# Seven block products for all eight expert pairs, with values read back from DRAM and gate logits laid over 128 partitions

## The chip, the core and the metric

The kernel runs on one core of a Trainium2 chip. Its engines are TensorE (PE, with its weight loads shown apart as PEld), VectorE (DVE), ScalarE (ACT), GpSimd (POOL) and SyncE (SP), which here issues every DMA. The engines run their own instructions in order and wait for each other by semaphores. SBUF is the on-chip memory with 128 partitions, PSUM the one that TensorE writes. The metric is the device time of one execution in microseconds; lower is better. Comparisons use the median of several runs and, where shown, a 95% interval.

## The reference

Eight sequences of 1,024 tokens with 256 features pass an attention layer without a softmax, a residual sum with a layer norm, and a mixture of 16 experts with a second residual sum and layer norm. All is float32. Cut to what matters:

```python
# x: (8, 1024, 256); Wqkv: (256, 768); keys: (16, 256, 128); values: (16, 128, 256)
q, k, v = split(x @ Wqkv + bqkv)
q2 = l2norm(q*q / (sum(q*q) + 1e-7), axis=-1)     # after the mean over features is taken off
k2 = l2norm(k*k / (sum(k*k) + 1e-7), axis=-2)
attn = (v + q2 @ (k2.T @ v) / sqrt(1024)) @ Wln + bln
x = layernorm(x + attn)
sel = sigmoid(x @ expert_sel.T)                    # (tokens, 16)
scores = relu(einsum('bsd,edh->bseh', x, keys))
out = einsum('bseh,ehv,bse->bsv', scores, values, sel)
x = layernorm(x + out)
```

## The kernel before

**Tiles.** The 8,192 tokens are worked in 16 chunks of 512 (`CH`). Features lie on partitions in two halves of 128. Each float32 operand is split into a high part, rounded to the type in which TensorE multiplies (`fp32r`), and the rest as a low part; a product then takes three matmuls, high by high, high by low, low by high (`passes3`). Names ending in h and l are such pairs: `ych`, `ycl` hold the input of the experts for a chunk, `keyh`, `keyl` the first layer's weights, `valh`, `vall` the second layer's, `sh`, `sl` the gated scores.

**The planner.** Nothing is written in the order in which it runs. Every operation is added with `add(engine, cost, key, fn, r, w)` as a task: a due time (`key`, about one unit for each expert), an estimate of its duration, and what it reads and writes. `Work.order` plays the program through with these costs and writes out one order for all engines; a task may start when its inputs are there, its slots are free and its key is at most `WINDOW` ahead of the oldest open task. Buffers come from slots with tags (`SB_SLOTS` in SBUF, `PS_SLOTS` in PSUM): a buffer takes a slot when the first task that touches it is placed and gives it back after the last one. At run time the engines follow that order and the semaphores. The constants `AT_...`, `EAGER`, `BOOST`, `LAG` set keys. TensorE is filled with short `warm` matmuls in the first stage where the planner has nothing for it.

**Stages.** The head makes the weights, the attention of chunk 0 and chunk 1 and the gates of the first experts. Then the steady part runs the 16 experts of chunk c, while the attention of the next chunks is worked in between: `u_y(c+1)` (queries, residual sum, gates), `u_q(c+2)`, `u_k(c+3)`, and `u_m` for the matrix of each sequence. `u_end` does the last layer norm of a chunk.

**The experts.** `u_pair(c, p)` does experts 2p and 2p+1. In the old way (`plain1`) an expert's first layer is 6 matmuls of 512 columns into one PSUM tile `h`. For chunks from 1 on and pairs in `FAST_PAIRS` (4 to 7), `fast1` computes both experts together: the two experts' keys and the two halves of the tokens are taken as a product of 2x2 blocks, which is done by seven block products in place of eight. Each product is 3 matmuls of 256 columns. It needs sums of key blocks (`sums_h`, `sums_l`, made once in `u_sums` by GpSimd) and sums of token blocks (`th`, `tl`, made for each chunk in `u_t`). The results are put together in two PSUM tiles `hx` and `hy`: products are accumulated, and ScalarE copies a partial sum from one half to another (L1099, L1100, L1103, L1106) before the next product is added; VectorE adds the last part (L1109). `gated` then does on either way: VectorE takes the maximum with zero and multiplies by the gate (L1055), ScalarE casts to the high part (L1056), VectorE subtracts for the low part (L1057). `ffn2` is the second layer, 6 matmuls of 512 columns for each expert (L1137) into two PSUM tiles that collect over all 16 experts.

**The gates.** In `u_y` the logits of 16 experts by 512 tokens are one row for each expert on 16 partitions (`gr`). The sigmoid is built of Exp, Ln and Newton steps: eight VectorE operations and six ScalarE operations on 16x512. The result is stored to DRAM (`sel`, L938), from where each expert's row is spread over 128 partitions (`selb`, L1030), two slots for two pairs.

**Slots.** Weights of experts sit in `g0` to `g3`, four slots each: key and value parts of four experts. `s4` has four slots for the split tokens and for k2 and q2, `t4` six for work tiles, among them `th` and `tl`. PSUM has four `h` slots: one tile for each expert in the old way, `hx` and `hy` for each pair in the other.

Of the kernel before, what the change touches and what calls it, by code (L numbers as in the profile page):

```python
# [15 lines left out]
P = 128  # L16
# [9 lines left out]
EARLY = 14  # L26
WARM = 14
WINDOW = 10.47
AHEAD = 120
HALVED = 4  # L30
FAST_FROM = 1
FAST_AT = 0.39
AT_Y, AT_YEND, AT_X, AT_N, AT_K, AT_Q, AT_M, AT_END = 2.04, 4.17, 0.95, 0.19, 5.21, 12, 16.28, -0.91
AT_Q1, AT_K2, AT_W1, AT_W2, AT_W3, AT_SUMS, AT_SEL = -30, -19.9, -10.93, -7.7, 8.8, 8.58, 7
EAGER = 3.73
BOOST = 2.0
RESERVE = {"att": 1}
FAST_PAIRS = range(4, 8)
# [3 lines left out]
    "ld2": 3, "xh": 2, "xl": 2, "s4": 4, "ych": 2, "ycl": 2, "sh": 2, "sl": 2, "selb": 2, "gt": 2, "t4": 6, "t2": 4,  # L42
    "v1": 2, "g0": 4, "g1": 4, "g2": 4, "g3": 4, "acc": 1, "asb": 1, "mh": 1, "ml": 1, "tiny": 14,
# [35 lines left out]
class Buf:  # L79
# [4 lines left out]
    def __getitem__(self, i):  # L84
        return self.ap[i]

# [236 lines left out]
def attn_ffn_kernel(ctx, tc, x, xT, wqT, wk, wvT, wlnT, bcols, brows, selT, keys, values, outT):  # L323
# [93 lines left out]
    keyh, keyl, valh, vall = {}, {}, {}, {}  # L417
# [99 lines left out]
    def split(c, key, name, src, h, l, width):  # L517

        rows = h.shape[1]
        n = 1 if c < 2 else 2  # L520
        for i in range(n):
            s = slice(i * rows // n, (i + 1) * rows // n)
            part = None if n == 1 else i
            b = sbuf("g3" if c < 2 else "ld2", [P, rows // n, width], f"{name}{c}_{i}")
            add("D", 2.1 / n, key, lambda b=b, s=s: nc.sync.dma_start(out=b.ap, in_=src(s)), w=[b])
            high(key + 1.2, lambda s=s: h[:, s], lambda b=b: b.ap, 2 * CH // n, [b], [(h, part)], c < 2)
            for j in range(2 // n):
                m = rows // 2
# [39 lines left out]
    def u_k(c, key):  # L568
# [5 lines left out]
        k2h[c] = h = sbuf(in_first(c, "s4", "ych"), [P, 4, D], f"k2h{c}", FR)  # L574
        k2l[c] = l = sbuf(in_first(c, "s4", "ycl"), [P, 4, D], f"k2l{c}", FR)
        for g in range(2):
# [7 lines left out]
            add("T", c_mm(D, 12), key + g, lambda g=g, t=t: project(c, g, t, wkh, wkl), r=x_parts(c, g) + [wkh, wkl], w=[t])  # L584
# [135 lines left out]
    def u_q(c, key):  # L720
        q = sbuf("t4", [P, 4, D], f"q{c}")
        s, n2, y, a = (tiny(f"{n}{c}") for n in ("qs", "qn", "qy", "qa"))
        q2h[c], q2l[c] = (sbuf("s4", [P, 2, CH], f"{t}{c}", FR) for t in ("q2h", "q2l"))
        for g in range(2):
# [7 lines left out]
            add("T", c_mm(D, 12), key + g, lambda g=g, t=t: project(c, g, t, wqh, wql), r=x_parts(c, g) + [wqh, wql], w=[t])  # L732
# [33 lines left out]
        for ct in range(2):  # L766
            o = psum(f"qt{c}_{ct}")

            def turn(ct=ct, o=o):
                for t in range(4):  # L770
                    T.transpose(o[:, t * P : (t + 1) * P], q[:, t, ct * P : (ct + 1) * P], ident.ap)  # L771

            add("T", c_mm(P, 4), key + 6.5 + ct * 0.2, turn, r=[q, ident], w=[o])
            add("S", c_act(CH, plain=True), key + 7 + ct * 0.2, lambda ct=ct, o=o: S.copy(q2h[c][:, ct, :], o.ap), r=[o], w=[(q2h[c], ct)])
            add("V", c_dve(CH), key + 7.5 + ct * 0.2, lambda ct=ct, o=o: V.tensor_tensor(
                q2l[c][:, ct, :], o.ap, f(q2h[c][:, ct, :]), ALU.subtract), r=[o, (q2h[c], ct)], w=[(q2l[c], ct)])
# [88 lines left out]
    def u_y(c, key):  # L865
# [18 lines left out]
        for jt in range(2):  # L884
            t = psum(f"yp{c}_{jt}", "h" if c == 0 else "att")
            k0 = key + jt
            add("T", c_mm(CH, 6), k0, lambda t=t, jt=jt: ymx(t, jt), r=[xh[c], xl[c], wyh, wyl] + ([] if c == 0 else [mh[b], ml[b], q2h[c], q2l[c]]), w=[t])
# [16 lines left out]
        def smm():  # L904
# [7 lines left out]
        gr = sbuf("t4", [P, 2, CH], f"gr{c}")  # L912
        a, z = lambda: gr[:NE, 0, :], lambda: gr[:NE, 1, :]
        rs = sbuf("t2", [P, CH], f"rs{c}")
        add("S", c_act(CH, plain=True), key + 0.5, lambda: S.copy(z(), z0[32 : 32 + NE, :]), r=[z0], w=[(gr, 1)])
        add("V", c_dve(CH), key + 1, lambda: V.tensor_tensor(z(), z0[:NE, :], z(), ALU.add), r=[z0, (gr, 1)], w=[(gr, 1)])

# [3 lines left out]
        key += 1.8  # L921

        add("S", c_act(CH), key, lambda: S.activation(a(), v[:NE], AF.Ln, bias=c_zero[:NE]), r=[v, c_zero], w=[(gr, 0)])
        add("S", c_act(CH), key + 0.1, lambda: S.activation(a(), a(), AF.Exp, bias=c_zero[:NE], scale=-0.5), r=[(gr, 0), c_zero], w=[(gr, 0)])
        newton(key + 0.4, lambda: v[:NE], a, lambda: rs[:NE], 1.0, [v, (gr, 0)], [rs, (gr, 0)])
        add("V", c_dve(CH), key + 0.8, lambda: V.tensor_tensor(z(), z(), a(), ALU.mult), r=[gr], w=[(gr, 1)], port=True)

        add("S", c_act(CH), key + 1.2, lambda: S.activation(z(), z(), AF.Exp, bias=c_zero[:NE], scale=-1.0), r=[(gr, 1), c_zero], w=[(gr, 1)])
        add("V", c_dve(CH, fast=True), key + 1.6, lambda: V.tensor_scalar(z(), z(), 2.0**62, 1.0, ALU.min, ALU.add),
            r=[(gr, 1)], w=[(gr, 1)], port=True)  # L930

        add("S", c_act(CH), key + 2, lambda: S.activation(a(), z(), AF.Ln, bias=c_zero[:NE]), r=[(gr, 1), c_zero], w=[(gr, 0)])
        add("S", c_act(CH), key + 2.1, lambda: S.activation(a(), a(), AF.Exp, bias=c_zero[:NE], scale=-1.0), r=[(gr, 0), c_zero], w=[(gr, 0)])
        add("V", c_dve(CH), key + 2.4, lambda: V.tensor_tensor(z(), z(), a(), ALU.mult), r=[gr], w=[(gr, 1)], port=True)
        add("V", c_dve(CH), key + 2.5, lambda: V.scalar_tensor_tensor(a(), z(), 2.0, a(), ALU.subtract, ALU.mult, reverse0=True),  # L935
            r=[gr], w=[(gr, 0)], port=True)
        selt[c] = d = work.buf("dram", [NE, CH], F32, f"sel{c}")
        add("D", 0.2, key + 2.8, lambda: nc.sync.dma_start(out=d.ap, in_=a()), r=[gr], w=[d])  # L938


    def u_weights(g, key):
        for to, name in ((keyh, "keyh"), (keyl, "keyl"), (valh, "valh"), (vall, "vall")):
            to[g] = sbuf(f"g{g}", [P, 4, 2, P] if to in (keyh, keyl) else [P, 4, D], f"{name}{g}", FR)
# [15 lines left out]
        for i in range(n):  # L959
# [10 lines left out]
            for j in range(size):  # L970
                e = here.start + j
                add("S", c_act(D), key + 1.4, lambda j=j, e=e, vst=vst, m=m: S.activation(valh[g][:, e], vst[:, j], AF.Identity, bias=m[:, j : j + 1]),
                    r=[vst, m], w=[(valh[g], e)])
                add("V", c_dve(D, ptr=True), key + 1.8, lambda j=j, e=e, vst=vst, m=m: V.scalar_tensor_tensor(
                    vall[g][:, e], vst[:, j], m[:, j : j + 1], f(valh[g][:, e]), ALU.add, ALU.subtract),
                    r=[vst, m, (valh[g], e)], w=[(vall[g], e)], port=True)
# [27 lines left out]
    def u_t(c, key):  # L1004
        yh, yl, n = ych[c], ycl[c], CH // 2
        y, u = sbuf("t4", [P, 2, CH], f"y{c}"), sbuf("t4", [P, 4, n], f"tu{c}")
        th[c], tl[c] = (sbuf("t4", [P, 4, n], f"t{i}{c}", FR) for i in "hl")
        for k in range(2):
            apply(key, lambda k=k: y[:, k], lambda k=k: f(yh[:, k]), lambda k=k: f(yl[:, k]), ALU.add, CH, [yh, yl], [(y, k)], "G")
# [5 lines left out]
        add("S", c_act(4 * n, plain=True), key + 1, lambda: S.copy(h.ap, u.ap), r=[u], w=[h])  # L1015
# [17 lines left out]
    def u_pair(c, p):  # L1033
# [3 lines left out]
        gates_of(c, p, max(0, SOON - 2 * p) if c == 0 else 0)  # L1037
        sel = selb[c, p]
# [74 lines left out]
    def ffn2_halves(c, e, key, a, b):  # L1113

        g, i = e // 4, e % 2
# [3 lines left out]
        def run(part):  # L1119
            r = slice(part * CH // 2, (part + 1) * CH // 2)  # L1120
            for j, (w, x) in enumerate(((valh[g], a), (vall[g], a), (valh[g], b))):
                for v in range(2):
                    out = rest[v][:, : CH // 2] if part else wps[c][v][:, r]
                    T.matmul(out, w[:, e % 4, v * P : (v + 1) * P], x[:, i, r], start=part == 1 and e == NE - HALVED and j == 0,
                             stop=e == NE - 1 and j == 2)

        for part in range(2):
            add("T", c_mm(CH // 2, 6), key + LAG + part * HALVED, lambda part=part: run(part),
                r=[(valh[g], e % 4), (vall[g], e % 4), (a, i), (b, i)], w=rest if part else wps[c])

    def ffn2(c, e, key, a, b):
        g, i = e // 4, e % 2

        def run():
            for j, (w, r) in enumerate(((valh[g], a), (vall[g], a), (valh[g], b))):
                for v in range(2):
                    T.matmul(wps[c][v].ap, w[:, e % 4, v * P : (v + 1) * P], r[:, i], start=e == 0 and j == 0, stop=e == NE - 1 and j == 2)  # L1137

        t = add("T", c_mm(CH, 6), key + LAG, run, r=[(valh[g], e % 4), (vall[g], e % 4), (a, i), (b, i)], w=wps[c])
# [3 lines left out]
    def u_end(c):  # L1143
# [3 lines left out]
        for v in range(2):  # L1147
            add("V", c_dve(CH), key, lambda v=v: V.tensor_tensor(w[:, v, :], wps[c][v].ap, f(ych[c][:, v, :]), ALU.add),  # L1148
                r=[wps[c][v], ych[c]], w=[(w, v)])
# [6 lines left out]
        yb = sbuf("t4", [P, 2, CH], f"wy{c}")  # L1156
# [249 lines left out]
```

## Time and profile before

| | |
|---|---|
| median of 3 runs | 1017.82 us (1015.98 to 1018.09) |
| the profiled execution, first to last instruction | 1013.8 us, mean granted TensorE clock 0.996 |
| program | 16,268 instructions |
| DMA | 99.52 MB, mean 98 GB/s, packets of the dynamic queue 30.4% of 16 engines' time |

The page of the profile gives busy time by engine, then the chain of work that ended last: it starts at the last instruction and goes back, at each step to what released it. Groups of instructions are shown as line, engine, operation, tile written <- tiles read, with a count and busy time, mean duration and the idle time before it. A matmul's duration is from its start to its modelled end and overlaps with the next, so a pace is read from starts. How much of each slice each engine was busy (digits are tenths) and the granted clock:

```profile
PE   9999999999999999999999999999999999999996
...
DVE  7889888588776887768887688867888688686775
ACT  7767576676776767767676676757776675665543
POOL 1001685538564474655636475454754537333430
PEclk9999999999999999999999999999999999999998
```

### The profile page before, as it was taken

What the parts mean: (1) busy time and instruction counts of PE and PEld (TensorE: products, weight loads), DVE (VectorE), ACT (ScalarE), POOL (GpSimd) and SP (SyncE); (2) the same over time, 40 slices, a digit from 0 to 9 for tenths busy, and PEclk for the clock granted to TensorE, in tenths of its full rate; (3) what the DMA queues carried; (4) which work ended last, traced back from release to release, by engine and by line L of the source; (5) the groups of instructions that cost most, each with busy time, mean ns of one, the idle gap of its engine ahead of it and who ended that gap; (6) DMA issues with size and microseconds to landing.
All of it is one profiled execution on the core that took longest, in us unless ns stands there. A gap on an engine that the chain in (4) does not pass through costs nothing.

```text
span 1013.8 us, 16268 instructions
## 1 busy us (share of the span) xinstructions
PE 1003.8 (99%) x5709; PEld 868.9 (86%) x5709; DVE 792.9 (78%) x1363; ACT 678.5 (67%) x1515; POOL 488.5 (48%) x436
## 2 busy tenths in 40 slices
PE   9999999999999999999999999999999999999996
PEld 9978879888898988889888888988889888888886
DVE  7889888588776887768887688867888688686775
ACT  7767576676776767767676676757776675665543
POOL 1001685538564474655636475454754537333430
PEclk9999999999999999999999999999999999999998
DMA  6144433322241333323223232323323222223131
GB/s 203 56 124 125 120 98 118 94 97 93 83 126 65 116 94 104 99 89 97 94 91 110 86 105 70 116 96 102 105 75 104 94 85 75 93 85 105 64 125 42
DMA packets 65298, 99.52 MB, mean 98 GB/s; under 512 B 6336, under 2 KB 24896, under 8 KB 65216
## 3 DMA queue, kind: packets, MB, share of 16 engines
q1 hardware_dynamic: 65216, 98.48, 30.4%
q8 instruction: 45, 0.74, 0.3%
q14 instruction: 37, 0.30, 0.1%
HBM read 89.54 MB, written 8.91 MB: 97 GB/s over the span
## 4 chain that ended last, share of the span: by engine, by line
PE 92%; DVE 3%; POOL 2%; DMA 1%; ACT 1%; issue 1%; SPq 0%; POOLq 0%; DVEq 0%; ACTq 0%
PE w L1137 32%; PE h L358 17%; PE hx L1090 11%; PE yp L358 8%; PE qp L358 4%; PE hy L1090 4%; PE kp L358 4%; PE ap L358 4%; PE qt L771 1%; PE sp L358 1%; PE pm L358 1%; DMA ksr<-keys 1%; PE warm L435 0%; DVE sl L1057 0%; DMA xf<-xT 0%
## 5 line engine op out<-in xcount | busy, mean ns | idle before, releaser
L1137 PE MATMUL w<-sh,valh 128*128 128x512 f32 x504 | 157.9, 394 | 0.0
L1137 PE MATMUL w<-sh,vall 128*128 128x512 f32 x504 | 157.8, 394 | 0.0
L1137 PE MATMUL w<-sl,valh 128*128 128x512 f32 x504 | 157.6, 394 | 0.0
L1055 DVE SCALAR_TENSOR_TENSOR h<-h,selb 128x512 f32<-128x512 f32 x136 | 93.9, 692 | 29.6 <-PE h L358 24.9
L1137 PEld LDWEIGHTS w<-sl,valh 128*128 128x128 f32 x504 | 94.6, 188 | 22.4
L1137 PEld LDWEIGHTS w<-sh,vall 128*128 128x128 f32 x504 | 94.6, 188 | 22.0
L1056 ACT CAST sh<-h 128x512 fp32r<-128x512 f32 x136 | 74.2, 588 | 57.2 <-PE w L1137 46.2
L358 PE MATMUL h<-ych,keyh 128*128 128x512 f32 x272 | 110.4, 406 | 0.0
L358 PE MATMUL h<-ycl,keyh 128*128 128x512 f32 x272 | 108.3, 398 | 0.0
L358 PE MATMUL h<-ych,keyl 128*128 128x512 f32 x272 | 107.5, 395 | 0.0
L1057 DVE TENSOR_TENSOR sl<-h,sh 128x512 fp32r<-128x512 f32 x136 | 87.7, 682 | 22.4 <-ACT sh L1056 22.3
L1137 PEld LDWEIGHTS w<-sh,valh 128*128 128x128 f32 x504 | 86.0, 188 | 10.9
L389 POOL TENSOR_TENSOR k<-k,ks 128x512 f32<-128x512 f32 x25 | 30.9, 1256 | 102.4 <-DVE ks L566 102.4
L1109 DVE TENSOR_TENSOR hx<-hx,p 128x512 f32<-128x512 f32 x60 | 41.8, 696 | 29.9 <-ACT hy L1106 29.6
L389 POOL TENSOR_TENSOR ysq<-ysq 128x512 f32<-128x512 f32 x15 | 20.0, 1333 | 89.2 <-ACT ysq L891 89.2
L1151 POOL TENSOR_TENSOR w<-w,ycl 128x512 f32<-128x512 f32 x30 | 38.3, 1297 | 49.4 <-DVE w L1148 49.4
L358 PEld LDWEIGHTS h<-ych,keyl 128*128 128x128 f32 x272 | 51.5, 189 | 12.2
L358 PEld LDWEIGHTS h<-ycl,keyh 128*128 128x128 f32 x272 | 51.6, 190 | 10.7
L358 PEld LDWEIGHTS h<-ych,keyh 128*128 128x128 f32 x272 | 51.5, 189 | 10.9
L893 DVE SCALAR_TENSOR_TENSOR ycl<-yp,by,ych 128x512 fp32r<-128x512 f32 x32 | 24.0, 750 | 41.4 <-ACT ysq L891 41.4
L389 POOL TENSOR_TENSOR kss<-kss 128x512 f32<-128x512 f32 (+1 forms) x18 | 25.0, 1391 | 57.6 <-DVE gr L935 57.6
L1057 DVE TENSOR_TENSOR sl<-hx,sh 128x512 fp32r<-128x512 f32 x60 | 40.8, 681 | 15.1 <-ACT sh L1056 14.9
(511 smaller groups left out, 3204.6 us busy)
## 6 DMA issues: line engine op xcount, KB each, us to landing
selb<-sel SPq DMA_DIRECT2D x253, 256.0 KB, 3.4
xf<-xT SPq DMA_DIRECT2D x30, 256.0 KB, 2.8
outT<-w SPq DMA_DIRECT2D x15, 512.0 KB, 3.0
nf<-x SPq DMA_DIRECT2D x28, 256.0 KB, 4.7
kst<-keys SPq DMA_DIRECT2D x6, 256.0 KB, 3.3
vst<-values SPq DMA_DIRECT2D x6, 256.0 KB, 3.0
nf<-x SPq DMA_DIRECT2D x2, 512.0 KB, 7.6
ksr<-keys SPq DMA_DIRECT2D x4, 256.0 KB, 3.6
```

The costliest lines, as they stand in the source:

```text
L358: T.matmul(out, w, r, start=first and i == 0, stop=last and i == len(terms) - 1)
L389: fns = {e: (lambda e=e: ENG[e].tensor_tensor(out(), a(), b(), op)) for e in engines}
L771: T.transpose(o[:, t * P : (t + 1) * P], q[:, t, ct * P : (ct + 1) * P], ident.ap)
L893: add("V", c_dve(CH, ptr=True), k0 + 0.9, lambda t=t, jt=jt: V.scalar_tensor_tensor(yl[:, jt, :], t.ap, by[:, jt : jt + 1], f(yh[:, jt, :] ...
L1055: add("V", c_dve(CH), key + 0.1, lambda: V.scalar_tensor_tensor(at(t.ap), at(h.ap), 0.0, out(sel), ALU.max, ALU.mult), r=[h] + reads(sel), ...
L1056: add("S", c_act(CH, plain=True), key + 0.1, lambda: S.copy(out(a), at(t.ap)), r=[t], w=reads(a))
L1057: add("V", c_dve(CH), key + 0.1, lambda: V.tensor_tensor(out(b), at(t.ap), f(out(a)), ALU.subtract), r=[t] + reads(a), w=reads(b))
L1090: T.matmul(out(), wi, ri, start=first and i == 0, stop=True, skip_group_check=True)
L1109: add("V", c_dve(CH), key + 0.09, lambda: V.tensor_tensor(halves_(x.ap), halves_(x.ap), p5.ap.to_broadcast([P, 2, n]), ALU.add), r=[x, p5] ...
L1137: T.matmul(wps[c][v].ap, w[:, e % 4, v * P : (v + 1) * P], r[:, i], start=e == 0 and j == 0, stop=e == NE - 1 and j == 2)
L1151: add("G", c_pool(CH), key + 0.5, lambda v=v: G.tensor_tensor(w[:, v, :], w[:, v, :], f(ycl[c][:, v, :]), ALU.add), r=[(w, v), ycl[c]], w= ...
```

## The change

Five things change together.

- `FAST_PAIRS` is `range(8)`: from chunk 1 on all eight pairs use `fast1`. `u_sums` makes key sums for eight pairs.
- Value weights no longer stay in SBUF. `u_weights` makes them for chunk 0 in tiles for one pair each (`vals`, tag `vs`, four slots) and stores each to DRAM (`vdram`); from chunk 1 on `u_pair` loads each pair's tile again, 512 KB, by SP. The slots of `g0` to `g3` go from four to two.
- The gate logits are moved by DMA into a tile of 128 partitions by 64 (16 experts by 8 pieces of 64 tokens), and so is the variance row `v`; the sigmoid runs on 128x64 and is stored from there.
- Slots are given out anew: `s4` becomes `nn` and `kq`, `th` and `tl` get `tf` (two slots) of their own, `t4` has four, and `u_end` uses one work tile twice. A mark `TAKE` lets a task reserve a slot that a later task writes; it adds no dependency between operations.
- The planner's constants have other values.

```diff
-EARLY = 14
+EARLY = 17.06
-WINDOW = 10.47
-AHEAD = 120
+WINDOW = 11.33
+AHEAD = 125.36
-FAST_AT = 0.39
-AT_Y, AT_YEND, AT_X, AT_N, AT_K, AT_Q, AT_M, AT_END = 2.04, 4.17, 0.95, 0.19, 5.21, 12, 16.28, -0.91
-AT_Q1, AT_K2, AT_W1, AT_W2, AT_W3, AT_SUMS, AT_SEL = -30, -19.9, -10.93, -7.7, 8.8, 8.58, 7
+FAST_AT = 8.9
+AT_Y, AT_YEND, AT_X, AT_N, AT_K, AT_Q, AT_M, AT_END = 2.49, 3.72, 6.25, -3.12, 10.31, 11.71, 15.9, -0.74
+AT_Q1, AT_K2, AT_W1, AT_W2, AT_W3, AT_SUMS, AT_SEL, AT_VALS = -31.56, -10.52, -6.89, 1.02, 6.34, 4.43, 7.02, 2.33
-BOOST = 2.0
+BOOST = 0.99
-FAST_PAIRS = range(4, 8)
+FAST_PAIRS = range(8)
 SB_SLOTS = {
-    "ld2": 3, "xh": 2, "xl": 2, "s4": 4, "ych": 2, "ycl": 2, "sh": 2, "sl": 2, "selb": 2, "gt": 2, "t4": 6, "t2": 4,
-    "v1": 2, "g0": 4, "g1": 4, "g2": 4, "g3": 4, "acc": 1, "asb": 1, "mh": 1, "ml": 1, "tiny": 14,
+    "ld2": 3, "xh": 2, "xl": 2, "nn": 2, "kq": 2, "ych": 2, "ycl": 2, "sh": 2, "sl": 2, "selb": 2, "gt": 2, "t4": 4, "tf": 2, "t2": 4,
+    "v1": 2, "g0": 2, "g1": 2, "g2": 2, "g3": 2, "vs": 4, "acc": 1, "asb": 1, "mh": 1, "ml": 1, "tiny": 14,
 }
...
+TAKE = -1
...
@@ u_y
-        add("S", c_act(CH, plain=True), key + 0.5, lambda: S.copy(z(), z0[32 : 32 + NE, :]), r=[z0], w=[(gr, 1)])
-        add("V", c_dve(CH), key + 1, lambda: V.tensor_tensor(z(), z0[:NE, :], z(), ALU.add), r=[z0, (gr, 1)], w=[(gr, 1)])
+        zc = sbuf("t2", [P, CH], f"zc{c}")
+        gt = sbuf("gt", [P, 6, CH // 8], f"gt{c}")
+        spread = lambda ap: ap.rearrange("e (t n) -> e t n", t=8)
+        eh, el, v8, a, rs, z = (lambda i=i: gt[:, i] for i in range(6))
+        m = CH // 8
+        add("S", c_act(CH, plain=True), key + 0.5, lambda: S.copy(zc[: 32 + NE], z0[: 32 + NE, :]), r=[z0], w=[zc])
+        for i in range(2):
+            add("D", 0.3, key + 0.7, lambda i=i: nc.sync.dma_start(out=gt[:, i], in_=spread(zc[32 * i : 32 * i + NE])), r=[zc], w=[(gt, i)])
...
+        add("D", 0.3, key + 1.7, lambda: nc.sync.dma_start(out=v8(), in_=spread(v[:NE])), r=[v], w=[(gt, 2)])
...
+        add("V", c_dve(m), key, lambda: V.tensor_tensor(z(), eh(), el(), ALU.add), r=[(gt, 0), (gt, 1)], w=[(gt, 5)], port=True)
+        add("S", c_act(m, 2), key, ln, r=[(gt, 2), c_zero], w=[(gt, 3)])
+        add("V", c_dve(m, 4), key + 0.2, logits, r=[(gt, 2)], w=[(gt, 3), (gt, 4), (gt, 5)], port=True)
+        add("S", c_act(m), key + 0.4, lambda: S.activation(z(), z(), AF.Exp, bias=c_zero.ap, scale=-1.0), r=[c_zero], w=[(gt, 5)])
+        add("V", c_dve(m), key + 0.5, lambda: V.tensor_scalar(z(), z(), 2.0**62, 1.0, ALU.min, ALU.add), w=[(gt, 5)], port=True)
+        add("S", c_act(m, 2), key + 0.6, inverse_, r=[(gt, 5), c_zero], w=[(gt, 3)])
+        add("V", c_dve(m, 2), key + 0.8, out, w=[(gt, 3), (gt, 5)], port=True)
         selt[c] = d = work.buf("dram", [NE, CH], F32, f"sel{c}")
-        add("D", 0.2, key + 2.8, lambda: nc.sync.dma_start(out=d.ap, in_=a()), r=[gr], w=[d])
+        add("D", 0.3, key + 0.9, lambda: nc.sync.dma_start(out=d.ap.rearrange("e (t n) -> (e t) n", t=8), in_=a()), r=[(gt, 3)], w=[d])
@@ u_weights
+        for p in (2 * g, 2 * g + 1):
+            vals[0, p] = sbuf("vs", [P, 2, 2, D], f"vals0_{p}", FR)
+            vdram[p] = work.buf("dram", [P, 2, 2, D], F32, f"vdram{p}")
...
+        for p in (2 * g, 2 * g + 1):
+            add("D", 2.1, key + 2.2, lambda p=p: nc.sync.dma_start(out=vdram[p].ap, in_=f(vals[0, p].ap)), r=[vals[0, p]], w=[vdram[p]])
@@ u_t
-        th[c], tl[c] = (sbuf("t4", [P, 4, n], f"t{i}{c}", FR) for i in "hl")
+        th[c], tl[c] = (sbuf("tf", [P, 4, n], f"t{i}{c}", FR) for i in "hl")
...
-        add("S", c_act(4 * n, plain=True), key + 1, lambda: S.copy(h.ap, u.ap), r=[u], w=[h])
+        add("S", c_act(4 * n, plain=True), key + 1, lambda: S.copy(h.ap, u.ap), r=[u], w=[h, (l, TAKE)])
@@ u_pair
+        if c:
+            vals[c, p] = sbuf("vs", [P, 2, 2, D], f"vals{c}_{p}", FR)
+            fetched[:] = [add("D", 2.1, key - AT_VALS, lambda: nc.sync.dma_start(out=f(vals[c, p].ap), in_=vdram[p].ap),
+                              r=[vdram[p]], w=[vals[c, p]], after=fetched)]
@@ ffn2
-            for j, (w, r) in enumerate(((valh[g], a), (vall[g], a), (valh[g], b))):
+            for j, (w, r) in enumerate(((0, a), (1, a), (0, b))):
                 for v in range(2):
-                    T.matmul(wps[c][v].ap, w[:, e % 4, v * P : (v + 1) * P], r[:, i], start=e == 0 and j == 0, stop=e == NE - 1 and j == 2)
+                    T.matmul(wps[c][v].ap, u[:, w, i, v * P : (v + 1) * P], r[:, i], start=e == 0 and j == 0, stop=e == NE - 1 and j == 2)
@@ u_end
-        yb = sbuf("t4", [P, 2, CH], f"wy{c}")
+        yb = sq
```

In the orders that the two programs are built to, TensorE has 816 matmuls of 512 columns of `h` before and 96 after, 1,260 of 256 columns of `hx` and `hy` before and 2,520 after, and 38 and 46 `warm` ones. SP issues 374 DMAs before and 551 after: 120 of `vals`, 8 of `vdram` and 45 of `gt` are new, and 4 more of `ksr`. Twelve halves of `tl` move from GpSimd to VectorE.

## The prediction

> **What bounds the kernel now.** I read the page's busy times and chain first, then the order of time on TensorE, then the groups and waits, last the DMA rows.
>
> ```profile
> PE 1003.8 (99%) x5709; PEld 868.9 (86%) x5709; DVE 792.9 (78%) x1363; ACT 678.5 (67%) x1515; POOL 488.5 (48%) x436
> PE 92%; DVE 3%; POOL 2%; DMA 1%; ACT 1%; issue 1%; SPq 0%; POOLq 0%; DVEq 0%; ACTq 0%
> ```
>
> The chain that ended last lies to 92% on TensorE. Busy time of pipelined matmuls says little, so I take the distance from one start to the next (first column of the order of time, us; chunk 8, a pair computed the old way, then one by block products):
>
> ```profile
> 552.88 0.39 PE L358 MATMUL h<-ych,keyh 128*128 128x512 f32 x1
> ...
> 554.04 0.39 PE L358 MATMUL h<-ych,keyl 128*128 128x512 f32 x1
> 554.27 0.63 PE L1137 MATMUL w<-sh,valh 128*128 128x512 f32 x2
> ...
> 576.02 0.28 PE L1090 MATMUL hx<-th,keyh 128*128 128x256 f32 x1
> ...
> 576.62 0.28 PE L1090 MATMUL hx<-ych,ksl 128*128 128x256 f32 x1
> 576.74 0.28 PE L358 MATMUL kp<-wkh,xh 128*128 128x256 f32 x1
> ```
>
> Six matmuls of 512 columns take 554.27-552.88 = 1.39 us, 232 ns each; six of 256 take 0.72 us, 120 ns each. Over the whole trace the starts of the second layer's 1,512 matmuls are 232.0 ns apart, and of all 5,708 distances those above the pace of their form add up to only 6.4 us, most of it before 65 us. So TensorE never waits in the steady part: the time is its work, and any TensorE work taken out comes off the span until something else is late.
>
> **The change, part by part.** *Block products.* Chunks 1 to 15 now do pairs 0 to 3 by L1090's seven products of 3 matmuls too: 15 x 4 = 60 pairs. Each loses 12 matmuls of 512 columns and gains 21 of 256. The 720 removed ones hold TensorE 169.6 us (235.5 ns each, their changes from transposes included); bare, at 232.0 ns, 167.0. The 1,260 present ones of 256 columns hold it 151.0 us (119.9 ns each, their waits included), and 60 pairs more cost the same again. Gain: 169.6-151.0 = 18.6 us; bare 16.0. I take 17, as part of the changes from transposes will fall on other matmuls.
>
> [...]
>
> *The chain inside a pair.* Between products ScalarE copies halves of PSUM, and TensorE needs other matmuls meanwhile. What one step needs (same pair of chunk 8):
>
> ```profile
> 572.70 0.28 PE L1090 MATMUL hx<-ych,keyl 128*128 128x256 f32 x1
> ...
> 573.81 0.39 PE L1090 MATMUL hx<-th,ksh 128*128 128x256 f32 x1
> ```
> ```profile
> 573.02 0.36 ACT L1099 COPY hy<-hx 128x256 f32<-128x256 f32 x1 [0.95 <-PE hx L1090]
> 573.38 0.37 ACT L1100 COPY p<-hx 128x256 f32<-128x256 f32 x1
> ```
>
> The last product starts at 572.70, ends 0.28 later, two copies follow 0.04 behind it, and the next product starts 0.06 after them: 1.11 us, so 1.11-0.12 = 1.0 us of other work hides it. Here four matmuls of 512 columns (0.93 us) lie between, and about 0.1 us shows. In the changed program's order I counted what lies there for every pair: 1.39 us at the median as before, but 0.71 to 0.76 in chunk 14 pairs 2 and 6 and chunk 15 pairs 0 and 1, and nothing in chunk 15 pair 2, where no attention work is left. That costs 4 x about 0.35 + 1.1 = 2.5 us. Bounds 1 (ScalarE is emptier there) and 5 (a 0.58 cast stands in front of each).
>
> *One set of th, tl.* They get their own two slots (tag tf), enough for one chunk, and the first pair now needs them, not the fifth. ScalarE's cast of th (L1015) waits for the last product of the old chunk, VectorE's tl follows.
>
> ```profile
> L1015 ACT CAST th<-tu 128x1024 fp32r<-128x1024 f32 x15 | 15.6, 1042 | 2.3 <-POOL tu L389 2.3
> L389 DVE TENSOR_TENSOR tl<-tu,th 128x512 fp32r<-128x512 f32 x16 | 17.3, 1089 | 1.0 <-ACT th L1015 1.0
> L389 POOL TENSOR_TENSOR tl<-tu,th 128x512 fp32r<-128x512 f32 x14 | 21.9, 1561 | 25.8 <-ACT th L1015 25.8
> ```
>
> Columns: busy us, mean ns | idle before. Counted from the start of that last product: ScalarE 0.32 to 1.36; VectorE first does hy's gate and a bias add (0.60 us apart when they follow each other), so tl's first half runs from 1.52 to 2.2, or 2.6 at 1,089 ns. In the changed order 6 matmuls of 512 and 12 of 256 columns lie between, 2.82 us, so tl is wanted at 0.12+2.82+0.12 = 3.06: hidden with 0.4 to 0.8 us over. Queued behind the cast are q's squares on ScalarE, behind tl the inverse of k's sums on VectorE, for which GpSimd's scaling of k waits; TensorE wants what comes of these only pairs later. Into chunk 15 just 1.39 us lie between: 0.32+1.04+0.04+(0.68 to 1.09)+0.06-1.63 = 0.5 to 0.9 us lost, I take 0.7. Its pair 1 also reuses PSUM 2.1 us after the pair two before has ended, where VectorE and ScalarE need 0.32 + two gates 1.2 + cast 0.58 + two subtractions 1.2, some overlapping, about 2.9: 0.8 us (0 to 2).
>
> *Other engines.* VectorE gains 60 adds (L1109, 696 ns): +42 us, and about 13 for 12 halves of tl that leave GpSimd. It loses the gate's eight operations on 16x512, 86 us in all, for eight on 128x64; these lie between the 128x4 rows (153 to 178 ns) and the 128x256 rows (471): 120 x 0.22 = 26 us, nearest the small ones. Net -5. ScalarE gains 60 x (361+371+364+358) ns = 87 us and 15 x 0.58 for zc, and loses 63 us of gate work for 75 x 0.3 = 22: net +55, to 734 us, 73%. GpSimd: -19 for tl, +15 for four more sets of key sums. None becomes the bound on average. The split of the slots (nn, kq, four of t4 for six) and the early reservations add no instruction; I cost them at nothing, since attention works one to three chunks ahead of the experts. Without that lead a late y would cost its own chain, about 2.7 us a chunk (two VectorE passes, a cast and a subtraction, 0.6 to 0.7 each).
>
> *DMA.* 120 loads of 512 KB of values, 8 stores of it, 45 small gate transfers.
>
> ```profile
> selb<-sel SPq DMA_DIRECT2D x253, 256.0 KB, 3.4
> outT<-w SPq DMA_DIRECT2D x15, 512.0 KB, 3.0
> nf<-x SPq DMA_DIRECT2D x28, 256.0 KB, 4.7
> nf<-x SPq DMA_DIRECT2D x2, 512.0 KB, 7.6
> sel<-gr SPq DMA_DIRECT2D x15, 32.0 KB, 1.7
> ```
>
> Last column: us from issue to landing. Bytes go from 99.5 to about 169 MB, 168 GB/s, with the DMA engines about half busy; the first slice already moved 203. In the changed order each load stands 14 to 29 us of TensorE work ahead of its first use and lands in 3.0 to 7.6: no cost. It waits on SP for the second layer four pairs back; behind it are the next gates (selb), issued 6 to 18 us ahead of use at 3.4 us landing. If that cover went, each late us would cost TensorE one. The small transfers of zc are issued 2.7 us or more ahead of VectorE's add, those of v1 2.1 to 3.8 (mean 2.9) ahead of ScalarE's Ln; at sel's 1.7 us they cost nothing.
>
> *Start.* Eight more warming matmuls stand in the head's order, two records of 0.112 us each: 1.8 us of further idle; bounds -2 (VectorE, 19 of 20 us busy from 20 to 40, has 7 instructions less there) and +3.5 (12 kp matmuls, 1.4 us, move behind it). I take 1.8.
>
> Sum: -17+2.5+0.7+0.8+1.8 = -11.2 us on this execution's 1013.8: 1002.6. The runs' median, 1017.8, stands 4.0 above that span, so **1007 us**. The low ends give -18.6+1+0.5+0-2 = -19.1, the high ends -16+5+0.9+2+3.5 = -4.6: its own range is 999 to 1013.
>
> **Rivals.** *The new wait takes the gain* (no change). If tl's second half counts, or VectorE is one operation late, a chunk boundary costs 1.52+1.09+1.09+0.06+0.69-3.06 = 1.4 us at most; 13 more of them cost 18: 1025 at worst, 1016 at half, which is the price I give it. For it: th and tl were ready some 30 us ahead and are not now. Against: TensorE is told of each half apart.
>
> *The gate's transfers hold ScalarE and VectorE* (slower). Both take instructions in order, so an Ln or an add waiting for 128 pieces of 256 bytes behind a 512 KB load holds the copies that the block products wait for. At nf's 4.7 us the Ln is 1.8 late, less the 0.4 that a step has over (1.39-1.0): 1.4 x 15 = 21 us, 1028. It decides from 11.2/15+0.4 = 1.1 us of lateness, a landing of 4.0 us. For it: the order leaves 2.9 us, and outT's 512 KB or a load of values goes out just before. Against: sel's 32 KB landed in 1.7. [...]
>
> *The values come late* (slower): SP in order behind a wait. One us for each eighth load is 15 us, 1022. The lead of 14 us speaks against it.
>
> **How the numbers follow.** Forecast 0.70; new wait 0.13; gate transfers 0.12; values 0.05. Within 0.2% (2 us, about what runs of this kernel can tell apart) I put 0.06, all from the new wait's half price, whose smaller prices give 0.05 of faster. Faster 0.75, slower 0.19. Range 998 to 1017: below it less than 0.05, above it most of the slower cases.
>
> **What would show it.** Right: 96 matmuls of h left, 2,520 of hx and hy at about 120 ns, no TensorE wait between chunks 2 and 14, a few us in chunk 15. Wrong: TensorE idle at each chunk's first hx on the cast of th or on tl, ScalarE's Ln on gt waiting for DMA each chunk, or w waiting for vals.

## The result and the profile after

The changed kernel takes 1024.86 us (median of 4 runs, 1023.06 to 1026.56); the kernel before, beside it on the same chip, 1016.9. The ratio is 1.0075, with a 95% interval of 1.0059 to 1.0091: slower by about 0.8%, where 1007 us was forecast. The profiled execution of the changed kernel has a span of 1021.8 us, 8.0 more than before.

From the page of the changed kernel, the busy times and the chain of work that ended last:

```profile
PE 1000.1 (98%) x6265; PEld 889.6 (87%) x6265; DVE 773.0 (76%) x1438; ACT 726.4 (71%) x1764; POOL 468.8 (46%) x444
...
PE 75%; DVE 10%; ACT 7%; DMA 5%; issue 2%; POOL 0%; SPq 0%; DVEq 0%; ACTq 0%
```

The averages moved the way that was forecast: ScalarE 726 us (734 said), VectorE 773 (788 said), no other engine near its limit. But the chain, 92% TensorE before, is 75% TensorE now; VectorE, ScalarE and DMA have come into it. TensorE is waiting again. How much, is read from the distances between the starts of its matmuls. I count as a wait what a distance has above the median of its form (232 ns for 512 columns, 118 for 256, 109 for transposes) where that is over 60 ns; sums in us, worked out from the order of time on TensorE:

| stretch of the trace | before | after | difference |
|---|---|---|---|
| start to 64 us | 8.1 | 9.0 | +0.9 |
| 64 to 160 us (chunks 0 and 1) | 1.7 | 7.5 | +5.8 |
| 160 to 935 us | 4.2 | 16.9 | +12.6 |
| 935 us to the end (chunk 15) | 1.3 | 5.4 | +4.2 |

The work itself shrank as planned: 1,260 matmuls of 256 columns at 118 ns in place of 720 of 512 at 232 ns are 148.7 - 167.0 = -18.4 us, and eight more warming matmuls +1.8. With +23.5 of waits that makes +6.9 of the 8.0. So nothing went wrong with the block products' arithmetic; the gain was paid out again in waits.

Who is waited for? In the views of waits (us in all, times, longest) only idle time after the modelled end of the matmul before counts, so the sums are smaller than the table's. The kernel before has one such wait of TensorE from 64 us to its end; most of the rest of its 7.1 us are distances about 0.1 us over the pace, without idle time:

```profile
PE hx L1090 <- ACT p L1100: 0.9, 1, 0.9
```

In the changed kernel, ScalarE's waits in the gate, and TensorE's own between 160 and 935 us and from 935 us to the end:

```profile
ACT gt L950 <- DVE gt L937: 12.8, 13, 1.3
ACT gt L932 <- DMA gt<-v: 11.3, 10, 2.2
```
```profile
PE hx L1117 <- ACT p L1127: 3.4, 7, 1.2
PE hy L1117 <- ACT hy L1133: 1.8, 3, 1.0
```
```profile
PE hx L1117 <- DVE sl L1084: 2.3, 3, 1.3
PE hy L1117 <- ACT hy L1126: 0.4, 1, 0.4
PE hx L1117 <- DVE tl L392: 0.3, 1, 0.3
```

In the steady part TensorE waits for ScalarE's copies inside the block products (L1127, L1133), and ScalarE itself has stood still in the gate, ten times for the transfer gt<-v. The DMA rows of the page say why (last column: median us from issue to landing):

```profile
selb<-sel SPq DMA_DIRECT2D x253, 256.0 KB, 3.8
vals<-vdram SPq DMA_DIRECT2D x120, 512.0 KB, 4.8
...
outT<-w SPq DMA_DIRECT2D x15, 512.0 KB, 6.6
...
gt<-zc SPq DMA_DIRECT2D x30, 32.0 KB, 2.1
...
gt<-v SPq DMA_DIRECT2D x15, 32.0 KB, 4.6
sel<-gt SPq DMA_DIRECT2D x15, 32.0 KB, 1.9
```

Three transfers have the same 32 KB; gt<-zc and sel land in about 2 us, gt<-v in 4.6 (medians). One case in the order of time, in chunk 3 (SP's queue, ScalarE, TensorE; start, us, in brackets the idle time before):

```profile
286.62 0.38 SPq L1063 DMA_DIRECT2D vals<-vdram  x1
287.10 0.39 SPq L1193 DMA_DIRECT2D outT<-w  x1
290.68 0.55 SPq L928 DMA_DIRECT2D gt<-v  x1
```
```profile
290.84 0.36 ACT L1126 COPY hy<-hx 128x256 f32<-128x256 f32 x1 [2.32 <-PE hx L1117]
...
295.28 0.35 ACT L932 ACTIVATE gt<-gt,c_zero 128x64 f32<-128x64 f32 x1 [1.77 <-DMA gt<-v]
295.67 0.35 ACT L933 ACTIVATE gt<-gt,c_zero 128x64 f32<-128x64 f32 x1
295.92 0.36 ACT L1133 COPY hy<-hx 128x256 f32<-128x256 f32 x1
```
```profile
295.46 0.28 PE L1117 MATMUL hx<-ych,keyl 128*128 128x256 f32 x1
296.33 0.39 PE L1117 MATMUL hy<-th,keyh 128*128 128x256 f32 x1 [0.60 <-ACT hy L1133]
```

512 KB of values and 512 KB of output were issued 4.1 and 3.6 us ahead of gt<-v on the same queue. ScalarE stands 1.77 us at Ln (L932), and the copy of L1133, which has nothing to do with the gate, comes behind it; TensorE's next step starts 296.33-295.46-0.12 = 0.75 us late. Ahead of twelve of the 15 transfers stand an outT, issued 1.2 to 4.1 us before, and a load of values. In eleven of these twelve gt<-v lands 0.16 to 0.18 us after that outT.

### The profile page after: what moved, and what is told of

It is laid out like the page before. It is cut to its first block, busy times and chain, and to the rows that moved or that the text cites. A ratio compares the mean times of both kernels' runs of the same rounds, so it can differ in the third digit from the quotient of the medians.

```text
span 1021.8 us, 18097 instructions
## 1 busy us (share of the span) xinstructions
PE 1000.1 (98%) x6265; PEld 889.6 (87%) x6265; DVE 773.0 (76%) x1438; ACT 726.4 (71%) x1764; POOL 468.8 (46%) x444
## 4 chain that ended last, share of the span: by engine, by line
PE 75%; DVE 10%; ACT 7%; DMA 5%; issue 2%; POOL 0%; SPq 0%; DVEq 0%; ACTq 0%
PE w L1164 26%; PE hx L1117 16%; PE yp L361 8%; PE hy L1117 7%; PE qp L361 4%; PE ap L361 4%; DMA gt<-v 3%; PE kp L361 2%; DVE sl L1084 2%; PE qt L775 1%; PE h L361 1%; PE pm L361 1%; DMA vals<-vdram 1%; DVE hx L1082 1%; PE warm L438 1%
## 5 line engine op out<-in xcount | busy, mean ns | idle before, releaser
L1164 PE MATMUL w<-sh,vals 128*128 128x512 f32 x1008 | 277.4, 397 | 1.2 <-DVE w L1175 1.2
L1164 PEld LDWEIGHTS w<-sh,vals 128*128 128x128 f32 x1008 | 173.8, 189 | 25.6 <-DVE w L1175 1.7
L1164 PE MATMUL w<-sl,vals 128*128 128x512 f32 x504 | 158.4, 395 | 0.0
L1084 DVE TENSOR_TENSOR sl<-hy,sh 128x512 fp32r<-128x512 f32 x120 | 82.5, 687 | 46.0 <-ACT sh L1083 44.4
L1164 PEld LDWEIGHTS w<-sl,vals 128*128 128x128 f32 x504 | 94.9, 188 | 22.7
L1082 DVE SCALAR_TENSOR_TENSOR hx<-hx,selb 128x512 f32<-128x512 f32 x120 | 83.5, 696 | 2.7
L1082 DVE SCALAR_TENSOR_TENSOR hy<-hy,selb 128x512 f32<-128x512 f32 x120 | 83.2, 693 | 1.9 <-PE hy L1117 1.8
L1133 ACT COPY hy<-hx 128x256 f32<-128x256 f32 x120 | 43.7, 364 | 48.0 <-PE hx L1117 47.4
L1126 ACT COPY hy<-hx 128x256 f32<-128x256 f32 x120 | 43.4, 362 | 47.9 <-PE hx L1117 45.2
L1117 PE MATMUL hx<-th,ksh 128*128 128x256 f32 x240 | 70.5, 294 | 6.0 <-ACT p L1127 3.4
L1083 ACT CAST sh<-hx 128x512 fp32r<-128x512 f32 x120 | 71.1, 592 | 0.2
```

Source lines behind the costliest of these rows:

```text
L1082: add("V", c_dve(CH), key + 0.1, lambda: V.scalar_tensor_tensor(at(t.ap), at(h.ap), 0.0, out(sel), ALU.max, ALU.mult), r=[h] + reads(sel), ...
L1083: add("S", c_act(CH, plain=True), key + 0.1, lambda: S.copy(out(a), at(t.ap)), r=[t], w=reads(a))
L1084: add("V", c_dve(CH), key + 0.1, lambda: V.tensor_tensor(out(b), at(t.ap), f(out(a)), ALU.subtract), r=[t] + reads(a), w=reads(b))
L1117: T.matmul(out(), wi, ri, start=first and i == 0, stop=True, skip_group_check=True)
L1126: add("S", c_act(n, plain=True), key + 0.02, lambda: S.copy(y0(), x1()), r=[x], w=[y])
L1133: add("S", c_act(n, plain=True), key + 0.07, lambda: S.copy(y1(), x1()), r=[x], w=[y])
```

## The experiments

Each run stands beside runs of the kernel before on the same chip (1016.1 us for e1 to e12, 1016.95 for e13 and e14), so ratios are compared; the changed kernel's is 1.0075. The diffs show of each line only the part that changes, with `...` between parts of the code. "Waits" are TensorE's from 64 us on, counted as in the table: 29.7 us after, 7.1 before.

**The transfers left out (e1).**

```diff
-add("D", 0.3, key + 1.7, lambda: nc.sync.dma_start(out=v8(), in_=spread(v[:NE])), r=[v], w=[(gt, 2)])
+add("D", 0.3, key + 1.7, lambda: None, r=[v], w=[(gt, 2)])
...
-S.activation(a(), v8(), AF.Ln, bias=c_zero.ap)
+S.activation(a(), v[:, :m], AF.Ln, bias=c_zero.ap)
```

> The 15 transfers gt<-v are left out; Ln and the Newton step of the gate read the first 64 columns of v in their place (so the gate's values are not the reference's), and every engine keeps its order. Theory 1, the gate's transfers hold ScalarE: its waits of 11.3 us before L932 go, and with them the TensorE waits right behind them (0.25+0.83, 0.76, 1.13, 0.44 us and the small ones after each): 4 to 10 us less, 1015 to 1021. Theory 2, eight block pairs in a row leave no slack for ScalarE whatever the gate does: within 2 us of 1024.9.

Measured: 1018.16 us, ratio 1.0018 (1.0008 to 1.0028). Theory 1's range. The waits between 160 and 935 us fall from 16.9 to 10.9; the other stretches stay. But 24.6 us of waits remain, so the transfers are one cause, not the only one.

**A later place in the order instead (e2).**

```diff
-r=[v], w=[(gt, 2)])
+r=[v], w=[(gt, 2)], late=2.5)
...
-t.done += self.LATENCY
+t.done += self.LATENCY + t.late
```

> All work is kept; the planner is told that gt<-v lands 2.5 us later than it thought, so Ln and what follows stand later in ScalarE's order. Theory 1: the same 4 to 10 us come back, 1015 to 1021, with the right gates. Theory 2: 1022 or more, since the same ScalarE operations stand somewhere else among the copies.

Measured: 1027.94 us, 1.0112 (1.0099 to 1.0125): slower than the change, outside theory 1's range. Ln no longer waits for the transfer, so that wait is cured; the planner however made another order of everything, with new waits (2.99 us at 143.8 us for a gated sl, 2.03 us in chunk 14), 35.1 us in all. This run says that a new order costs as much as the wait that it removes, and nothing about theory 2.

**The old gate in the new kernel (e3).** The gate block of the kernel before in place of the new one.

```diff
-zc = sbuf("t2", [P, CH], f"zc{c}")
-gt = sbuf("gt", [P, 6, CH // 8], f"gt{c}")
...
+gr = sbuf("t4", [P, 2, CH], f"gr{c}")
+a, z = lambda: gr[:NE, 0, :], lambda: gr[:NE, 1, :]
```

> The gate as before (16 partitions x 512, no gt transfers), all else of the change kept. Theory 1: no Ln waits for a DMA, 1022 or less. Theory 2: the old gate's four ScalarE operations of 0.72 us and its waits for VectorE (18.9 us before) hold the copies at least as much as the new one's: 1025 or more, up to 1045 if each of its 15 chains costs a step more than now.

Measured: 1087.21 us, 1.0698 (1.0675 to 1.0721), far beyond both. Waits of 93 us, the largest group of them for sl of the pair two before (longest 3.3 us). The old gate also takes one of the four slots of t4, so its long operations and the lost slot are not separated here. What follows is only that, with these slots and the order that the planner then makes, the gate can't be undone alone.

**Pairs 0 to 3 back to the plain form (e4).**

```diff
-FAST_PAIRS = range(8)
+FAST_PAIRS = range(4, 8)
```

> Pairs 0 to 3 go back to the plain form, all else of the change kept: TensorE's work grows by 16 to 18.6 us. Theory 1 (the gate's chain falls on pairs 6 and 7, which stay block products): the waits stay, 1024.9+17.5-(0 to 5) = 1037 to 1042. Theory 2: the waits go with the slack that plain pairs give, 1024.9+17.5-(10 to 15) = 1027 to 1032.

Measured: 1042.89 us, 1.0263 (1.0244 to 1.0282): 0.0188, or 19 us, above the change, 0.5 us over the top of theory 1's sum (1024.9+17.5 = 1042.4). The waits are 29.7 us as before the edit, but not the same ones: now yp waits for q2l in most chunks (0.5 to 0.9 us by the starts) and hx of pair 4 for a copy that stands behind a cast waiting for GpSimd. So the number came close in part for a wrong reason. What it does show, the sums of waits being equal: the block products of the four pairs are worth 19 us, and the rest of the change (layout of the gate, slots, constants, streaming) costs 1042.9-1016.1 = 27 us without them.

**gt<-v first in the queue (e5).** After the order is made, gt<-v is put ahead of outT and vals issued up to 6 us before it.

```diff
+for t in [t for t in order if t.ahead == 1]:
+    for x in [x for x in order if x.ahead == -1 and 0 <= t.start - x.start < BEHIND]:
+        i, j = order.index(x), order.index(t)
...
+            order.insert(j, order.pop(i))
```

> All work is kept; in the order of SP's queue each gt<-v goes ahead of the outT store and the load of values that were issued up to 6 us before it; no other engine's order changes. Theory 1 as it stands now (gt<-v lands 4.6 us after issue because 1 MB is ahead of it in the queue): it lands in about 2 us and the time is that of the run without these transfers, 1016 to 1021. Rival (the 128 pieces of 256 bytes are slow by themselves): it still lands in 4 us or more, 1023 to 1027.

Measured: 1018.83 us, 1.0028 (1.0018 to 1.0038). In the page of this run, and on its SP queue and ScalarE at the same place in chunk 3:

```profile
outT<-w SPq DMA_DIRECT2D x15, 512.0 KB, 3.4
...
gt<-v SPq DMA_DIRECT2D x15, 32.0 KB, 2.0
```
```profile
289.15 0.56 SPq L929 DMA_DIRECT2D gt<-v  x1
289.76 0.58 SPq L1194 DMA_DIRECT2D outT<-w  x1
```
```profile
291.86 0.36 ACT L933 ACTIVATE gt<-gt,c_zero 128x64 f32<-128x64 f32 x1
292.25 0.35 ACT L934 ACTIVATE gt<-gt,c_zero 128x64 f32<-128x64 f32 x1
293.53 0.36 ACT L1134 COPY hy<-hx 128x256 f32<-128x256 f32 x1 [0.93 <-PE hx L1118]
```

The same 128 pieces of 256 bytes land in 2.0 us; Ln starts unhindered, and the copy now waits for TensorE, as it should. The rival (small pieces are slow) falls. Nothing but the order in one queue was changed (the instructions of the other engines stand in the same order in both traces), and the ratio drops by 0.0047, about 5 us. This shows the mechanism, with all work kept.

**No reloading of values (e6).**

```diff
-lambda: nc.sync.dma_start(out=f(vals[c, p].ap), in_=vdram[p].ap)
+lambda: nc.sync.dma_start(out=f(vals[c, p].ap), in_=vdram[p].ap) if c == 1 else None
```

> The values of chunks 2 to 15 are not loaded again: 112 loads of 512 KB are left out, and the second layer uses what the four slots hold from chunk 1 (not the reference's values); all other engines keep their order. Theory 1: streaming costs only through what stands ahead of gt<-v (only outT is left): 1017 to 1022. Theory 3, streaming costs by itself (bandwidth, SP in order): below 1015. If it costs nothing at all: 1023 to 1026.

Measured: 1019.5 us, 1.0034 (1.0021 to 1.0046), no better than e5, though the bytes fall from 169 to 111 MB. The rows of outT and gt<-v in this run:

```profile
outT<-w SPq DMA_DIRECT2D x15, 512.0 KB, 3.7
...
gt<-v SPq DMA_DIRECT2D x15, 32.0 KB, 2.6
```

From chunk 2 on only outT is ahead: where it was issued 1.2 us before, gt<-v lands in 2.6 to 2.9 us, where 3.8 us before, in 2.0. So streaming 59 MB costs what it puts in front of the gate, about 4 us, and nothing else that these runs can tell.

**Chunk 15 in the plain form (e7).**

```diff
-if c >= FAST_FROM and p in FAST_PAIRS:
+if c >= FAST_FROM and p in (FAST_PAIRS if c < NCHK - 1 else range(4, 8)):
```

> Chunk 15 does pairs 0 to 3 in the plain form as before the change; the planner makes a new order. TensorE's work grows by 4 x 0.28 = 1.1 us. If the 5.4 us of waits in chunk 15 come from block products without attention work to fill the steps, 4 of them go: 1021 to 1023. If they come from the new constants, they stay: 1025 to 1027.

The four plain pairs of chunk 15 use, for half of their second key, the difference that the block form keeps in its place, so chunk 15's values are not the reference's; the work is that of the plain form. Measured: 1019.75 us, 1.0037 (1.0023 to 1.0051), 4 us below the change, better than expected. The waits after 935 us fall from 5.4 to 1.0, those elsewhere stay (6.5 and 16.7). The constants are the same, and TensorE, VectorE and ScalarE run the same order as in the changed kernel up to 958 us, where chunk 15 begins. So the waits of chunk 15 came from block products without filling work.

**The new gate in the kernel before (e8), and its control (e12).** e8 has the gate block of the changed kernel and t4 cut to 5 slots; e12 only the cut.

```diff
-"t4": 6
+"t4": 5
...
-gr = sbuf("t4", [P, 2, CH], f"gr{c}")
+zc = sbuf("t2", [P, CH], f"zc{c}")
+gt = sbuf("gt", [P, 6, CH // 8], f"gt{c}")
```

> The kernel before with the gate on 128 partitions and its transfers alone (the slots t4 go from 6 to 5 for room; values stay in SBUF, four pairs by block products). Theory 1: gt<-v falls behind outT here too, some copies of pairs 4 to 7 come late: 1017 to 1022. If the new gate's shorter operations are a gain where no values are streamed: 1015 or less.

> The kernel before with t4 cut from 6 to 5 slots and nothing else: the control for the run of the new gate in the kernel before (1024.6). If that run's 8.5 us came from the gate's transfers and short operations: 1015 to 1018 here. If they came from the lost slot and the new order that it makes: 1020 to 1025.

Measured: e8 1024.58 us, 1.0078 (1.0065 to 1.0091); e12 1016.65, 1.0002 (0.9993 to 1.0011). The slot costs nothing; the new gate, in the order that the planner then makes, costs the kernel before 8 us. But not as theory 1 said: gt<-v lands in 3.3 us here (mostly 0.2 us after two loads of selb issued just ahead of it) and Ln waits five times, 4.1 us in all, with little behind it. The wait is at ap, in nearly every chunk. VectorE, GpSimd and TensorE in e8:

```profile
291.62 1.35 DVE L940 SCALAR_TENSOR_TENSOR gt<-gt 128x64 f32<-128x64 f32 x1
292.89 0.68 DVE L1069 TENSOR_TENSOR sl<-hy,sh 128x512 fp32r<-128x512 f32 x1
293.49 0.68 DVE L389 TENSOR_TENSOR k2l<-k,k2h 128x512 fp32r<-128x512 f32 x1
```
```profile
291.59 1.30 POOL L389 TENSOR_TENSOR k<-k 128x512 f32<-128x512 f32 x1 [0.69 <-DVE gt L939]
```
```profile
294.22 0.38 PE L358 MATMUL ap<-k2l,nh 128*128 128x256 f32 x1
```

An operation on 128x64 that takes 0.23 us alone takes 1.35 us here; it starts 0.03 us after GpSimd's addition of 1.30 and ends shortly after it. In all 12 chunks in which it overlaps with an operation of GpSimd it takes 1.34 to 1.35 us, in the other three 0.23. k2l comes 1.1 us later for it, and TensorE stops at ap (0.29 us by the starts, 0.3 to 0.5 in most chunks). These stops and the matmul behind them make 5.4 of the 8 us; that they come from this operation is read from the trace, no run moves it. Here a short operation in front of a long queue cost more than its length: 0.23 us alone, 1.1 us of delay for k2l.

**Both cures (e9), the gate's second half later too (e10).** e9 is e5 with chunk 15 plain, and four 64 KB loads in chunk 14 bring back the half keys, so the output is the reference's. e10 also moves Exp (L950) and what follows it in the gate 1.1 us back in every engine's order.

```diff
+def u_back(p, key):
...
+    add("D", 0.4, key, lambda: nc.sync.dma_start(out=b.ap, in_=keys[2 * p + 1, :P, :]), w=[b])
+    add("S", c_act(P, plain=True), key + 2, lambda: S.copy(keyh[g][:, e, 0], b.ap), r=[b], w=[(keyh[g], one)])
...
-r=[c_zero], w=[(gt, 5)])
+r=[c_zero], w=[(gt, 5)], ahead=1.1)
...
+order = [t for _, _, t in sorted((t.start + (t.ahead if t.ahead not in (-1, 0, 1) else 0), i, t) for i, t in enumerate(order))]
```

> Both cures together, with the reference's keys: gt<-v goes first on SP's queue, and chunk 15 does pairs 0 to 3 in the plain form (the four half keys that the block form had changed are loaded again in chunk 14). If the two losses are separate, the gains add: 1018.8 - (1024.9 - 1019.8) = 1013.7, and up to 1 more for the loads: 1013 to 1015, below the kernel before. If the order of the whole is what matters, the sum is lost: 1016 or more.

> As the run with both cures, and the second half of the gate's chain (Exp, min, Ln, Exp, the last two products, sel) stands 1.1 us later in every engine's order. If the 0.33 us waits of every even chunk come from Exp (L951) waiting 1.07 us for VectorE's Newton step ahead of the copies, 7 of them and the 1.2 us at 105.6 us go: 2 to 4 us less than the run with both cures. If the copies wait for something else: within 1 us of it or above it.

Measured: e9 1015.05 us, 0.9989 (0.9979 to 0.9998); e10 1013.15 us, 0.9969 (0.9957 to 0.9980). The gains add (1.0075 - 0.0047 - 0.0038 = 0.9990), and e10, at the low edge of its expectation, takes 2 us more. ScalarE in chunk 8 of the changed kernel, then the same place in e10:

```profile
596.43 0.35 ACT L933 ACTIVATE gt<-gt,c_zero 128x64 f32<-128x64 f32 x1
597.85 0.35 ACT L950 ACTIVATE gt<-gt,c_zero 128x64 f32<-128x64 f32 x1 [1.07 <-DVE gt L937]
598.11 0.36 ACT L1133 COPY hy<-hx 128x256 f32<-128x256 f32 x1
```
```profile
590.80 0.35 ACT L934 ACTIVATE gt<-gt,c_zero 128x64 f32<-128x64 f32 x1
592.07 0.36 ACT L1142 COPY hy<-hx 128x256 f32<-128x256 f32 x1 [0.93 <-PE hx L1126]
```

Exp no longer stands in front of the copy, and the six waits of 0.33 us at pair 7 of the even chunks are gone. The wait of 1.2 us at 105 us stayed (1.16), against the expectation. TensorE's waits between 160 and 935 us in e10 are, in the form shown above for the changed kernel:

```profile
PE hx L1126 <- DVE sl L1093: 0.4, 1, 0.4
PE hy L1126 <- ACT hy L1142: 0.2, 1, 0.2
PE hx L1126 <- ACT p L1136: 0.2, 1, 0.2
```

e10 is below both kernels.

**The start (e11, e13, e14).** e11 gives chunk 1 plain pairs 0 to 3 too and makes their key sums in chunk 1. e13 is e10 with two things moved at the start (VectorE's four operations on 128x2 in the first matrix step behind the two adds of w; the casts of the key sums behind the copies). e14 is e13 with chunk 15's gate where the planner had it.

```diff
-(FAST_PAIRS if c < NCHK - 1 else range(4, 8))
+(FAST_PAIRS if 1 < c < NCHK - 1 else range(4, 8))
...
-mnewt, r=[kn, ky], w=[ka, ky])
+mnewt, r=[kn, ky], w=[ka, ky], ahead=3 if b == 1 else 0)
...
-S.copy(h.ap, u[:, three]), r=[u], w=[h])
+S.copy(h.ap, u[:, three]), r=[u], w=[h], ahead=0.8)
...
-ahead=1.1)
+ahead=1.1 if c < NCHK - 1 else 0)
```

> As the run with both cures, and chunk 1 also does pairs 0 to 3 in the plain form, their sums of keys being made in chunk 1 and not in chunk 0. TensorE's work grows by 1.1 us. If the 6 us more of waits between 64 and 160 us come from block products and eight sets of sums in the crowded start, 3 to 6 of them go: 2 to 5 us less in all. If they come from the new constants and slots: 0 to 2 us more.

> As the run with the gate's chain later (1013.15), and at the start only: VectorE's four operations on 128x2 of the first matrix step (L366 to L689, which took 0.39 to 0.96 us each while GpSimd formed key sums) go behind the two adds of w of chunk 0, and ScalarE's casts of the key sums go behind the copies they stood before. If the waits at 122.6 us (0.96, behind the casts) and at 140.9 and 142.1 us (0.61, 0.97, behind the small operations) come from eight sets of key sums in chunks 0 and 1, 1.5 to 2.5 us go: 1010.6 to 1011.7. If what stands next is late anyway: 1013 or more.

> As the run before it, with the gate of chunk 15 back where the planner had it. The waits that moving it had put into chunk 14 (0.26, 0.41 and 0.57 us) go: about 1 us less than the run before it; within 0.5 if they have another cause.

Measured: e11 1020.24 us, 1.0036 (1.0024 to 1.0048), 5 us above e9; the planner's new order has 16.1 us of waits in the steady part where e9 has 11.0, and 7.9 between 64 and 160 us, so neither of its two explanations is tested. e13 1012.72, 0.9962 (0.9948 to 0.9975), and e14 1014.43, 0.9971 (0.9960 to 0.9982): neither can be told from e10. In e13 the waits at 122.6 and 142 us shrink (0.96 to 0.36; 0.61 and 0.97 to 0.39 at the second alone), and new ones of 1.27 and 0.67 us stand at 139.0 and 144.9: what stood next was late too. Both expectations failed: e13 lies between its two ranges, and e14 above both of its own.

## Why the prediction was wrong

**Block products, -17 us: right.** -18.4 by the new median of 118 ns; e4 puts the four pairs at 19 us. The 96 matmuls of h are left, and the mean distance of hx and hy is 125.1 ns, of which 118 is the bare pace and the rest waits.

**The gate's transfers "at sel's 1.7 us they cost nothing": the step that failed.** They were priced by the row with the same size. gt<-v landed in 4.6 us, because what decides is not its size but when the 1 MB issued just before it lands: 4.6 behind vals and outT, 2.6 behind outT alone (e6), 2.0 in front of both (e5). Nor was the row of 1.7 us taken on an empty queue: in twelve of its 15 cases sel stood behind two selb loads of 256 KB, but these had been issued 2.0 and 2.4 us earlier, and the later of them landed 1.4 to 1.7 us after sel's issue. The lead of 2.9 us was about right in the odd chunks (up to 2.9, most of them over 2.4); in the even ones from chunk 2 to 12 Ln came about 6 us after the issue. The rival had the mechanism, nf's 4.7 us as the landing, and the 512 KB in front as the point for it; it should have had the higher chance, since the order showed those transfers ahead. The landings follow that order: in eleven of the twelve cases with outT ahead, gt<-v landed 0.16 to 0.18 us after that outT; what holds it until then, no run shows. The rival's price was too high, 1028: Ln waited 11.3 us in ten chunks, but TensorE lost only about 5 of it, since in most even chunks the 6 us left room.

**The gate's chain, not priced at all.** Its operations were costed by their sum on each engine (0.22 us on VectorE was right, 0.30 on ScalarE is 0.35), not as a chain in which ScalarE waits for VectorE: L950 waits 12.8 us in 13 chunks. Moving it is worth 2 us (e10).

**The chain inside a pair, +2.5, th and tl, +0.7, reuse of PSUM, +0.8: the sum and chunk 15 right, the split not.** Chunk 15 lost 4.2 us where these three make 4.0, and e7 gives them back; that the sum fits is in part luck. By the starts, with the matmul behind each wait, tl cost 0.7 as set. The chain shows once there, 0.7 us for a copy (L1126), and in chunk 14 once more, 0.3. Three waits for sl of an earlier pair, that is for PSUM to come free, cost 3.0 us where 0.8 was set. Since tl shows at no other chunk boundary of the steady part, the rival of a new wait at every one falls.

**In the steady part no wait was set for the chain, since 1.39 us of other work lay in its steps at the median.** Even with both cures and the later gate (e10) TensorE waits 5.7 us more there than before, in pieces of at most 0.6 us; of those over 0.12 us most are for copies. What makes these copies late is open.

**Start, +1.8: right up to the first second-layer matmul** (63.07 to 64.71 us), but nothing was set for chunks 0 and 1 behind it, which lost 5.8 us, in single waits of up to 1.1. Its cause was looked for with e11 and e13 and not settled: moving waits there moved them on. That the key sums of eight pairs lie beside it is only argued.

**Values, zero: right for the second layer, wrong for the queue.** No matmul of w waits for vals, and e6 gains nothing over e5; but the loads stand ahead of gt<-v, and without them (e6) 4 us come back.

In the sum: the forecast span, 1002.6 us, and the measured one, 1021.8, are 19.2 us apart. Both terms of the gate were set at nothing, and runs show 5 us for the place in the queue and 2 for the chain; 5.8 us between 64 and 160 us and the 5.7 of the steady part are open. The same 5 and 2, with 4 for chunk 15, make up the changed kernel's distance to e10, 10.8 us.

## What to carry to other kernels

Price a small transfer by when what stands ahead of it on its queue lands, not by its size (here the same 32 KB landed in 4.6 us behind 1 MB, in 2.0 ahead of it), and look at the issue order before choosing the row. Once another engine's short steps stand between TensorE's matmuls, price every operation put on that engine by what waits behind it (in chunk 3 the 1.77 us that ScalarE stood at Ln made TensorE's next step 0.75 us late). And where a planner makes the whole order, compare versions that move one thing in the finished order (e5, e10): a newly planned order can move the time by several us, whatever was edited (e2 came 3 us above the change, e11 5 us above e9).

## What the runs showed of the hardware

In the changed kernel a wait cost more than itself: the first matmul of 256 columns after a wait is followed by the next start 0.22 us later, not 0.12 (36 waits of more than 0.15 us, median 0.104 us more). It can be seen above at 296.33, whose duration is 0.39 for 0.28.

In chunk 15 of e5 waits of 1.52 and 0.61 us were followed by matmuls at about half pace; shown are the windows of 966 to 969 and 969.1 to 971.6 us (busy time of TensorE, its weight loads, VectorE, ScalarE, GpSimd, then granted clock, DMA share, GB/s), then the window behind the same two waits (1.49, 0.61) in the changed kernel:

```profile
966.00:969.00 3.00, 1.88 (x12) 1.71 (x13) 2.92 (x5) 1.20 (x4) 1.20 (x1) 0.93 0.85 254
969.10:971.60 2.50, 2.50 (x8) 2.01 (x7) 0.00 (x0) 1.66 (x3) 2.50 (x3) 0.50 0.57 196
```
```profile
972.60:976.00 3.40, 2.87 (x17) 2.52 (x18) 2.32 (x4) 1.51 (x4) 2.19 (x2) 1.00 0.80 269
```

Six matmuls of 512 columns took 427 ns each in the one (granted clock 0.50), 232 in the other (1.00): 1.2 us lost or not behind waits that differ by 0.03 us. What decides between the two, no run here shows.
